# Layer 2 of a four-layer convolution stack: the 17x17 box filter as a running sum on VectorE and one banded matmul, with the squares on ScalarE

## The chip, the cores and the metric

The kernel runs on one core of a Trainium2 chip. A core has a matrix engine (TensorE, in the profile PE for the matmuls and PEld for the loads of the stationary operand), a vector engine (VectorE, DVE), an engine for pointwise functions (ScalarE, ACT), GpSimd (POOL) and SyncE (SP), which here only starts transfers. Each engine runs its own instructions in order, and the engines wait for each other by semaphores. Operands lie in an on-chip memory of 128 partitions (SBUF); TensorE writes its results into PSUM, eight banks of 128 x 512 float32 numbers. The metric is the time of one execution in microseconds (us); lower is better.

## The reference

The input is x, four images of 16 channels of 512 x 512 float32 numbers. Four layers follow each other, and each is `x = x + conv(groupnorm(x))` with its own kind of convolution. Groupnorm has eight groups of two channels, with mean and variance over the group's two whole planes. Layer 0 is a block of dilated convolutions, layer 1 a quantized 3 x 3 convolution, layer 3 a convolution of the two-dimensional spectrum. Layer 2, the one at issue, is a box filter of every channel by itself:

```
k = 2 * r + 1                                  # r = 8, k = 17
kx = full((C, 1, 1, k), 1/k);  ky = full((C, 1, k, 1), 1/k)
x = conv(x, kx, padding=[(0, 0), (r, r)], feature_group_count=C)   # along rows
x = conv(x, ky, padding=[(r, r), (0, 0)], feature_group_count=C)   # down columns
...
x = x + _L2_conv_ref(_gn(x), 8)
```

So every output is the mean of a 17 x 17 neighbourhood of the normalised plane, with zeros beyond the edges, and the plane itself is added to it.

## The kernel before, in words

The layers run one after the other and hand their results over through scratch arrays in DRAM: layer 2 reads `x2` and writes `x3`. Layer 2 is the function `layer2`. It walks over 64 planes, i = 16 b + c for image b and channel c. A plane of 512 x 512 lies in SBUF as a tile of 128 partitions by 4 by 512: partition p and block k hold row 128 k + p.

Per plane there are these steps. `load` brings 1 MB from `x2` (line 1171, tile l2x, four buffers). `normal` applies the scale and bias of the group on ScalarE (line 1177, tile l2n). `first` and `second` each make the sum of 17 in one direction, and both do it with the helper `box` (line 1159): the data are the stationary operand, 128 x 128 at a time, and a band matrix `c_band` of 128 x 144 is streamed through; a matmul contracts over partitions, so the result comes out transposed. `first` therefore yields the transposed plane, summed down its columns; ScalarE copies it from PSUM (line 1188, tile l2y). `second` sums the other direction and turns the plane back. Each pass has four output blocks of four matmuls, and a float32 matmul is two instructions in the profile, so a plane takes 64 matmul instructions on line 1159. For each of its four blocks `second` then adds the plane on VectorE straight from PSUM (line 1199, tile l2o) and takes mean and variance of the sum (line 1200, `bn_stats`); every second plane line 1203 merges them into the group's entry of `mv`. One transfer stores the plane to `x3` (line 1201).

`column_sums` serves layer 3: four matmuls with the three columns of `c_cs` (line 1210) sum the finished plane over its rows with the weights 1, cos and sin, on four strips of 32 columns of the array; ScalarE copies the result (line 1214), and three small transfers store it (line 1216).

The order of the work is written out by hand (`manual_schedule`): what the loop at the end of `layer2` calls first, each engine does first. In round i these are: load plane i+3, `first` of plane i+1, `normal` of plane i+2, `column_sums` of plane i-1, `second` of plane i. Two rounds after the end of an image `group_stats` reduces the image's statistics over the partitions with two small matmuls (line 902) and a chain of short VectorE operations; after the second image `edges` prepares rows for layer 3, one step per round (`advance`). In PSUM the two passes have two banks each, the column sums one, the statistics one, the edge rows two.

Of the kernel before, what the change touches and what calls it, by code (L numbers as in the profile page):

```python
# [13 lines left out]
F32 = mybir.dt.float32  # L14
AF = mybir.ActivationFunctionType
ALU = mybir.AluOpType
AX = mybir.AxisListType
PSUM = bass.MemoryType.PSUM
DRAM = bass.MemoryType.DRAM

P = 128
B, C, H, W = 4, 16, 512, 512
NYB = H // 8
G = 8
# [19 lines left out]


R = 8
BAND = P + 2 * R


HW = W // 2  # L50
# [2 lines left out]
def shape_constants():  # L53

    k = {}
    p = np.arange(P)


    sel = np.zeros((P, G), np.float32)
    sel[p, p % C // 2] = 1  # L60
    k["c_sel_g"] = sel


    k["c_frame_is"] = (p // 4 % 4)[:, None] == np.arange(4)[None]
    k["c_parity"] = (p // 8 % 2)[:, None] == np.arange(2)[None]


    j = np.arange(BAND)
    k["c_band"] = np.where(np.abs(p[:, None] - (j[None] - R)) <= R, np.float32(1.0 / (2 * R + 1)), np.float32(0))


    n = W
    th = 2 * np.pi / n
    i = np.arange(n)
    half = np.arange(n // 2)
    split = np.concatenate([half[0::2], half[1::2]])

    def fold(v):
        lo, hi = v[..., split], v[..., split + n // 2]
        return np.concatenate([lo + hi, lo - hi], -1)  # L80

    cos, sin = np.cos(th * i), np.sin(th * i)
    q = np.stack([np.ones(n), cos, sin], -1)
    k["c_cs"] = np.ascontiguousarray(q.reshape(4, P, 3).transpose(1, 0, 2))
    hk = (2.0 / n) * np.sin(th * (np.outer(np.arange(1, n // 2), i) % n)).sum(0)
    d = (half[None, :] - half[:, None]) % n
    hil = [-(hk[d] + s * hk[(d + n // 2) % n]) for s in (1, -1)]
    k["c_hil"] = np.stack([h[1 - o :: 2, o::2] for h in hil for o in range(2)], 1)
    k["c_tab"] = np.broadcast_to(np.stack([cos, sin])[:, split], (P, 2, n // 2))
    y = 2 * np.arange(4)[None] + (p // C % 2)[:, None]  # L90
    k["c_ycs"] = np.stack([cos[y], sin[y]], 1)
    k["c_pair"] = (p // C % 2)[:, None] == np.arange(2)[None]
    k["c_eye"] = (p % C)[:, None] == np.arange(C)[None]
    k["c_ident"] = np.eye(P)
    bg = np.arange(NBG)[None]
    k["c_sel_bg"] = (bg == p[:, None] // 32 * G + p[:, None] % C // 2) * 1.0
    of = (p[:, None] // 32 == np.arange(B)[None]) / n
    k["c_bmask"] = np.stack([-of, of], 1)


    g = p // C % 4
    re = np.array([[1, 0, 0, 0], [0, 1, 0, 0], [0, 0, 1, 0], [0, 0, 0, -1]])
    im = np.array([[0, 1, 0, 0], [-1, 0, 0, 0], [0, 0, 0, 1], [0, 0, 1, 0]])
    k["c_edge_f"] = np.concatenate([re, im], 1)[g]
    k["c_edge_mask"] = (4 * (p // 64) + np.array([0, 1, 2, 2])[g])[:, None] == p[None] // C
    k["c_edge_sum"] = (g[:, None] < 2) * 1.0
    k["c_third"] = (g[:, None] == 2) * 2.0 * n
    first = (i == 0) * 1.0
    v = np.stack([-cos / n, -sin / n, -np.ones(n) / n, first])
    of = (np.arange(C)[None, :] == (p % C)[:, None])[None, :, None, :]  # L110
    k["c_lc"] = (v[g].reshape(P, NYB, 8).transpose(1, 0, 2)[..., None] * of).reshape(NYB, P, P)
    row = np.zeros((P, 2, n))
    row[g == 3, 0] = fold(first)
    row[g == 3, 1] = -fold(hk)
    k["c_bias_row"] = row
    return {name: np.ascontiguousarray(a, dtype=np.float32) for name, a in k.items()}
# [738 lines left out]
class Kernel:  # L855
# [43 lines left out]
    def across(self, psum, tag, ones, val, n):  # L899

        ps = psum.tile([P, n], F32, name=f"ps_{tag}", tag="gn_ps")
        self.nc.tensor.matmul(ps, ones, val, start=True, stop=True)
        t = self.small.tile([P, n], F32, name=f"ac_{tag}", tag=f"gn_{tag}")
        self.nc.vector.tensor_copy(t, ps)
        return t
# [230 lines left out]
    def layer2(self, x2, x3, sums, gn, l3):  # L1136
        tc, nc = self.tc, self.nc
        res, under_way = [], []
        with ExitStack() as ctx:
            wpool = ctx.enter_context(tc.tile_pool(name="l2w", bufs=1))  # L1140
            xin = ctx.enter_context(tc.tile_pool(name="l2x", bufs=4))
            work = ctx.enter_context(tc.tile_pool(name="l2work", bufs=2))
            edge = ctx.enter_context(tc.tile_pool(name="l2edge", bufs=1))
            ps1 = ctx.enter_context(tc.tile_pool(name="l2p1", bufs=2, space=PSUM))
            ps2 = ctx.enter_context(tc.tile_pool(name="l2p2", bufs=2, space=PSUM))
            pc = ctx.enter_context(tc.tile_pool(name="l2p3", bufs=1, space=PSUM)).tile([P, W], F32, name="l2p3")
            gps = ctx.enter_context(tc.tile_pool(name="l2gps", bufs=1, space=PSUM))
# [1 line left out]
            nc.vector.memset(pc, 0.0)  # L1149
            band, cs = l3.band, l3.cs  # L1150
            mv = wpool.tile([P, B, G, 2], F32, name="mv3")
            xts, xns, yts, outs = {}, {}, {}, {}

            def box(ps, lhs, at):

                for k in range(4):
                    lo, hi = max(0, P * k - R), min(W, P * k + P + R)
                    j = lo - (P * k - R)
                    nc.tensor.matmul(  # L1159
                        ps[:, lo:hi],  # L1160
                        lhs[:, k, at : at + P],
                        band[:, j : j + hi - lo],
                        start=(k == 0),
                        stop=(k == 3),
                        skip_group_check=True,
                    )

            def load(i):
                b, c = divmod(i, C)
                xts[i] = xin.tile([P, 4, W], F32, name=f"l2x_{i}", tag="x")  # L1170
                nc.sync.dma_start(xts[i], x2[b][:, c, :].rearrange("(k p) w -> p k w", p=P))

            def normal(i):
                b, c = divmod(i, C)
                g = c // 2
                xns[i] = work.tile([P, 4, W], F32, name=f"l2n_{i}", tag="xn")
                nc.scalar.activation(  # L1177
                    xns[i], xts[i], AF.Identity, bias=gn[b][1][:, g : g + 1], scale=gn[b][0][:, g : g + 1]
                )

            def first(i):

                xn = xns.pop(i)
                yts[i] = work.tile([P, 4, H], F32, name=f"l2y_{i}", tag="yt")
                for wb in range(4):
                    ps = ps1.tile([P, H], F32, name=f"l2p1_{i}_{wb}", tag="ps")
                    box(ps, xn, wb * P)
                    nc.scalar.copy(yts[i][:, wb, :], ps)  # L1188

            def second(i):  # L1190
                b, c = divmod(i, C)
                yt, xt = yts.pop(i), xts.pop(i)
                o = outs[i] = work.tile([P, 4, W], F32, name=f"l2o_{i}", tag="o", bufs=3)
                if c % 2 == 0:
                    self.st = self.small.tile([P, 2, 4, 6], F32, name=f"st3_{i}", tag="st3")
                for hb in range(4):
                    ps = ps2.tile([P, W], F32, name=f"l2p2_{i}_{hb}", tag="ps")
                    box(ps, yt, hb * P)
                    nc.vector.tensor_add(o[:, hb, :], xt[:, hb, :], ps)  # L1199
                    nc.vector.bn_stats(self.st[:, c % 2, hb, :], o[:, hb, :])  # L1200
                nc.sync.dma_start(x3[b][:, c, :].rearrange("(k p) w -> p k w", p=P), o)
                if c % 2 == 1:
                    nc.vector.bn_aggr(mv[:, b, c // 2, :], self.st.rearrange("p i r s -> p (i r s)"))

            def column_sums(i):

# [11 lines left out]
            def advance():  # L1218
                for e in list(under_way):
                    if next(e, None) is None:  # L1220
                        under_way.remove(e)
# [4 lines left out]
            n = B * C  # L1226
            with tc.manual_schedule():
                for i in range(3):
                    load(i)
                normal(0)  # L1230
                first(0)
                normal(1)
                for i in range(n + 1):
                    if i + 3 < n:
                        load(i + 3)
                    if i + 1 < n:
                        first(i + 1)
                    if i + 2 < n:
                        normal(i + 2)
                    if i > 0:  # L1240
                        column_sums(i - 1)
                    if i < n:
                        second(i)
                    advance()
                    if i > C and i % C == 1 or i == n:
                        b = (i - 1) // C - (i < n)
                        res.append(self.group_stats(gps, self.stats, f"x3_{b}", mv[:, b], G))
                        if b == 1:
                            under_way.append(self.edges(l3, 0, res, sums, tiles, *eps))
# [548 lines left out]
```

## Time and profile before

| | |
|---|---|
| median of 3 runs | 5003.81 us (4993.23 to 5010.5) |
| the profiled execution | 5009.29 us, span 5007.5 us |
| TensorE busy over the span | 4718.3 us, 94% |
| VectorE busy | 4028.1 us, 80% |
| ScalarE busy | 2558.2 us, 51% |
| layer 2, first normalisation to last addition | 3361.4 to 3998.0 us of the span |
| granted clock of TensorE, mean over the span | 0.977 |

The profile is of one execution. Its page gives the busy time of each engine, the chain of work that ended last, and groups of instructions: line, engine, operation, what is written and read by the program's names with partitions x elements, the count, and then busy time and mean duration in nanoseconds, and the idle time of the engine just before them with what ended it. A time line, the chain in order of time, and sums over chosen windows can be asked of the same trace. Matmuls overlap, so the duration of one matmul is longer than the distance to the next. The granted clock is the share of TensorE's full clock that the chip allowed in that time.

Durations of layer 2 before, each from its row: line 1177 2097 ns for 2048 elements, line 1188 586 ns, line 1199 675 ns, line 1200 695 ns, line 1203 372 ns, line 1214 575 ns.

### The profile page before, as it was taken

To read this page: it belongs to the slowest core of one execution; us is meant where nothing else is said; L and a number is where in the kernel's file an instruction comes from. 1 tells how busy PE (TensorE), PEld (TensorE's weight loads), DVE (VectorE), ACT (ScalarE), POOL (GpSimd) and SP (SyncE) were. 2 spreads that over 40 slices of the span, in tenths; PEclk is the share of its full clock that TensorE was granted. 3 is DMA by queue.
4 is the path that set the end of the run, shared out by engine and by line. 5 is a ranking of instruction groups with operands and counts; after the bars stand their busy time and mean duration, and the time that the engine had idled before them with its cause. 6 is when DMAs were issued, how large, how long until landed. Compare 5 with 4: busy or idle time off the path is not lost.

```text
span 5007.5 us, 200506 instructions
## 1 busy us (share of the span) xinstructions
PE 4718.3 (94%) x90224; PEld 2669.6 (53%) x90224; DVE 4028.1 (80%) x4031; ACT 2558.2 (51%) x4156; POOL 21.4 (0%) x90
## 2 busy tenths in 40 slices
PE   4899999999999999989989699989999989999999
PEld 1344444444444444434434345548888767777776
DVE  8888888979779899899899666655555588888887
ACT  3465656563324443444434555545444456666665
POOL 0000000000000000000000000000000000000000
PEclk9999999999999999999999899999999999999999
DMA  5656665563577677776875688866666655555553
GB/s 174 167 159 168 173 167 158 154 177 99 120 143 157 151 158 158 155 161 145 163 151 134 171 267 271 266 227 228 215 215 203 208 137 148 149 143 141 152 147 115
DMA packets 393819, 850.64 MB, mean 170 GB/s; under 512 B 70912, under 2 KB 86400, under 8 KB 384512
## 3 DMA queue, kind: packets, MB, share of 16 engines
q1 hardware_dynamic: 385456, 827.22, 61.9%
q8 instruction: 707, 11.58, 1.1%
q10 hardware_dynamic: 7504, 10.60, 0.8%
q14 instruction: 152, 1.25, 0.1%
HBM read 497.51 MB, written 340.03 MB: 167 GB/s over the span
## 4 chain that ended last, share of the span: by engine, by line
PE 79%; DVE 12%; DMA 3%; issue 3%; ACT 2%; SPq 1%; ACTq 0%; POOL 0%; DVEq 0%; POOLq 0%
PE m L592 41%; PE l1p L1052 10%; PE l2p L1159 8%; PE u L1627 5%; PE s L1568 5%; PE u L1568 4%; DVE frame L500 3%; PE u L1590 2%; PE pt L1602 2%; DVE l2o L1199 2%; PE l2p L1210 1%; DVE frame L445 1%; DVE st L1200 1%; DMA frame<-y 1%; DVE B L641 1%
## 5 line engine op out<-in xcount | busy, mean ns | idle before, releaser
L592 PE MATMUL m<-frame,l0w 32*64 32x512 f32 (+1 forms) x55296 | 2609.5, 611 | 176.1 <-DVE frame L540 63.3
L592 PEld LDWEIGHTS m<-frame,l0w 32*64 32x64 f32 (+1 forms) x55296 | 1178.6, 119 | 1606.0 <-issue 1389.4
L500 DVE SCALAR_TENSOR_TENSOR frame<-frame,frame 128x2376 f32<-128x2376 f32 x232 | 607.9, 2629 | 8.6
L1052 PE MATMUL l1p<-l1q,l_wt 32*32 32x512 f32 (+1 forms) x9216 | 429.6, 604 | 48.0 <-DVE l1q L1039 41.5
L1199 DVE TENSOR_TENSOR l2o<-l2x,l2p 128x512 f32<-128x512 f32 x256 | 172.8, 675 | 263.6 <-PE l2p L1159 263.6
L714 ACT ACTIVATE junk<-xb,neg 128x1024 f32<-128x1024 f32 x256 | 294.1, 1149 | 85.4 <-issue 42.6
L1052 PEld LDWEIGHTS l1p<-l1q,l_wt 32*32 32x32 f32 (+1 forms) x9216 | 189.9, 113 | 249.8 <-issue 209.5
L1159 PEld LDWEIGHTS l2p<-k_c_band,l2y 128*128 128x128 f32 x2048 | 256.7, 190 | 75.8 <-issue 55.0
L1188 ACT COPY l2y<-l2p 128x512 f32<-128x512 f32 x256 | 150.0, 586 | 280.7 <-PE l2p L1159 280.7
L1159 PE MATMUL l2p<-k_c_band,l2y 128*128 128x144 f32 (+1 forms) x2048 | 284.2, 292 | 6.1
L445 DVE STREAM_TRANSPOSE frame<-xp 128x1056 f32<-128x1056 f32 x128 | 261.2, 2124 | 29.7 <-ACT xp L414 29.7
L1159 PE MATMUL l2p<-k_c_band,l2n 128*128 128x144 f32 (+1 forms) x2048 | 266.6, 290 | 13.8 <-DMA l2x<-x 6.8
L1159 PEld LDWEIGHTS l2p<-k_c_band,l2n 128*128 128x128 f32 x2048 | 260.1, 195 | 14.5 <-ACT l2n L1177 12.2
L1627 PE MATMUL u<-k_c_hil,zt 128*128 128x128 f32 x2048 | 255.9, 278 | 0.0
L1627 PEld LDWEIGHTS u<-k_c_hil,zt 128*128 128x128 f32 x2048 | 238.4, 192 | 2.1 <-issue 0.8
L1603 ACT COPY zt<-pt 128x512 f32<-128x512 f32 x256 | 131.4, 599 | 208.2 <-PE pt L1602 208.2
L1533 DVE TENSOR_TENSOR xc<-l3n,k_c_tab 128x2048 f32<-128x2048 f32 x64 | 146.7, 2293 | 107.6 <-ACT l3n L1517 107.6
L1067 ACT ACTIVATE l1o<-l1p,k_l_bias,l_osc 128x1024 f32<-128x1024 f32 x128 | 147.2, 1201 | 144.8 <-PE l1p L1052 139.3
L1646 DVE SCALAR_TENSOR_TENSOR l3o<-u,l3t 128x256 f32<-128x256 f32 x512 | 192.5, 427 | 22.3 <-ACT l3t L1638 19.5
L1069 DVE BATCH_NORM_STATS2 l1st<-l1o 128x6 f32<-128x512 f32 x256 | 158.2, 681 | 54.4 <-ACT l1o L1067 54.2
L1052 PE MATMUL l1p<-l1x,l_wt 32*32 32x512 f32 (+1 forms) x3064 | 195.0, 593 | 0.0
L1033 ACT ACTIVATE l1t<-l1x,l1own,l1own 128x1024 f32<-128x1024 f32 x128 | 151.8, 1234 | 81.4 <-DMA l1x<-x 76.5
(313 smaller groups left out, 6256.7 us busy)
## 6 DMA issues: line engine op xcount, KB each, us to landing
y<-y SPq DMA_DIRECT2D x256, 264.0 KB
xb<-in_x SPq DMA_DIRECT2D x512, 128.0 KB
x<-l1o SPq DMA_DIRECT2D x256, 256.0 KB
l2x<-x SPq DMA_DIRECT2D x64, 1024.0 KB
x<-l2o SPq DMA_DIRECT2D x64, 1024.0 KB
l3x<-x SPq DMA_DIRECT2D x256, 256.0 KB
out<-l3o SPq DMA_DIRECT2D x256, 256.0 KB
l1x<-x SPq DMA_DIRECT2D x252, 256.0 KB
```

Of the source, the lines that this page charges most:

```text
L445: nc.vector.transpose(v[:, :, :, h, 1:17].rearrange("p k u m -> p k m u"), xp)
L500: self.nc.vector.scalar_tensor_tensor(o, x, f, y, ALU.mult, ALU.add)
L592: return nc.tensor.matmul(ps[at, i, :].rearrange("p (k c m) -> p k c m", k=nc_, c=2), w[PX * i : PX * i + PX, weights], source(i, d, e, j) ...
L714: nc.scalar.activation(junk, xs[:, h], f, bias=neg, accum_out=self.out_sums[b][n][:, 2 * t + h : 2 * t + h + 1])
L1033: nc.scalar.activation(t[:, at], x[:, at], AF.Identity, bias=own[1], scale=own[0])
L1052: ins = nc.tensor.matmul(ps[at : at + hi - lo, b, :], wt[rows, d, lo:hi], qs[v % 3][rows, k, d : d + W] if d < 3 else raws[v][rows, k], st ...
L1069: nc.vector.bn_stats(st[b][:, u, :], o[:, b, :])
L1159: nc.tensor.matmul(ps[:, lo:hi], lhs[:, k, at : at + P], band[:, j : j + hi - lo], start=(k == 0), stop=(k == 3), skip_group_check=True,)
L1199: nc.vector.tensor_add(o[:, hb, :], xt[:, hb, :], ps)
L1568: nc.tensor.matmul(ps[b][32 * j : 32 * j + 32], f[rows, n, j, :], x[rows, j, :], start=(i == 0), stop=(i == 2 and tag == "s"), skip_group_ ...
L1627: nc.tensor.matmul(po[:, bass.ts(k, P)], zt[:, b, k ^ 1, :], hil[:, k, :], start=False, stop=(k == 3), skip_group_check=True,)
L1646: nc.vector.scalar_tensor_tensor(o[:, v].rearrange("p k u -> p u k"), po[:, HW:W].rearrange("p (u k) -> p u k", u=2), s, t.rearrange("p (u ...
```

## The change

Layer 2 alone is changed; the rest of the program stays.

- Along the rows: `normal` writes into one of three tiles that are set to zero once. Each of the four rows of a partition takes 520 places there, 512 numbers and 8 zeros, with 17 zeros ahead of the first. `across` makes one VectorE instruction, `tensor_tensor_scan`, over 2080 places: the running value plus the number at this place, minus the number 17 places back. That is the sum of the last 17 numbers; read 8 places later it is centred.
- Down the columns: `down` keeps the band matrix, now 128 x 192 with both factors 1/17 in it, as the stationary operand and streams the row sums, 512 columns at a time. Four full matmuls take the blocks of 128 rows; six of 32 x 32 bring in the 8 rows from the neighbouring block. Nothing is transposed. The two halves of the result lie in two PSUM tiles of two banks each, with two such tiles in all, so the next plane uses the same ones. A plane has 20 matmul instructions here.
- `second` adds the plane with two `tensor_tensor_reduce` instructions of 1024 elements, which also give the sum of the output. ScalarE makes the squares (`Square`, shifted by an approximate mean, with an accumulator) in place of the four copies. `statistics` turns the sums into mean and variance once per image, with six small VectorE operations, in place of `bn_stats` and its merging.
- The order of a round is now: load plane i+3, `normal` of plane i+2, `second` of plane i (with its matmuls), `column_sums` of plane i-1, `across` of plane i+1.

```diff
-            def box(ps, lhs, at):
-                for k in range(4):
...
+            neg = wpool.tile([P, B, G], F32, name="l2neg")
+            for b in range(B):
+                nc.vector.reciprocal(neg[:, b], gn[b][0])
+                nc.vector.tensor_mul(neg[:, b], neg[:, b], gn[b][1])
+            padded = [wpool.tile([P, 2 * R + 1 + 4 * STEP], F32, name=f"l2n_{i}") for i in range(3)]
+            for xn in padded:
+                nc.vector.memset(xn, 0.0)
...
-            def first(i):
...
-                    box(ps, xn, wb * P)
-                    nc.scalar.copy(yts[i][:, wb, :], ps)
+            def across(i):
+                xn = padded[i % 3]
+                h = hs[i] = work.tile([P, 4 * STEP], F32, name=f"l2h_{i}", tag="h")
+                nc.vector.tensor_tensor_scan(
+                    h, xn[:, 2 * R + 1 :], xn[:, 0 : 4 * STEP], 0.0, ALU.add, ALU.subtract
+                )
+
+            def down(i):
+                x = hs.pop(i).rearrange("p (k w) -> p k w", w=STEP)[:, :, R:STEP]
+                ps = [ps2.tile([P, 2, W], F32, name=f"l2p2_{i}_{n}", tag="ps") for n in range(2)]
+                full = slice(0, P)
+                order = [(k, k, full, 32, full) for k in range(4)]
+                for k in range(3):
+                    order.append((k, k + 1, slice(P - 32, P), P + 32, slice(0, 32)))
+                    order.append((k + 1, k, slice(0, 32), 0, slice(P - 32, P)))
+                for k, to, rows, at, out in order:
+                    m = out.stop - out.start
+                    nc.tensor.matmul(ps[to // 2][out, to % 2, :], band[rows, at : at + m], x[rows, k, :],
+                        start=(m == P), stop=True, skip_group_check=True)
+                return ps
...
             def second(i):
...
-                for hb in range(4):
-                    ps = ps2.tile([P, W], F32, name=f"l2p2_{i}_{hb}", tag="ps")
-                    box(ps, yt, hb * P)
-                    nc.vector.tensor_add(o[:, hb, :], xt[:, hb, :], ps)
-                    nc.vector.bn_stats(self.st[:, c % 2, hb, :], o[:, hb, :])
+                for n in range(2):
+                    v = slice(2 * n, 2 * n + 2)
+                    nc.vector.tensor_tensor_reduce(
+                        o[:, v], xt[:, v], ps[n], 1.0, 0.0, ALU.add, ALU.add, s1[:, c, n : n + 1]
+                    )
                 nc.sync.dma_start(x3[b][:, c, :].rearrange("(k p) w -> p k w", p=P), o)
-                if c % 2 == 1:
-                    nc.vector.bn_aggr(mv[:, b, c // 2, :], self.st.rearrange("p i r s -> p (i r s)"))
+                junk = work.tile([P, 4, W], F32, name=f"l2j_{i}", tag="j", bufs=1)
+                nc.scalar.activation(
+                    junk, o, AF.Square, bias=neg[:, b, c // 2 : c // 2 + 1], accum_out=s2[:, c, 0:1]
+                )
...
-                    if i + 1 < n:
-                        first(i + 1)
                     if i + 2 < n:
                         normal(i + 2)
+                    if i < n:
+                        second(i)
                     if i > 0:
                         column_sums(i - 1)
-                    if i < n:
-                        second(i)
+                    if i + 1 < n:
+                        across(i + 1)
+                    if i % C == C - 1:
+                        statistics(i // C)
                     advance()
```

## The prediction

> **What bounds the kernel now.** I read the page first (spans, busy shares, the chain), then cut out the stretch of layer 2 by windows, then the chain inside that stretch, then the groups by shape for prices, and at last short windows around a pause for the granted clock.
>
> ```profile
> span 5007.5 us, 200506 instructions
> PE 4718.3 (94%) x90224; PEld 2669.6 (53%) x90224; DVE 4028.1 (80%) x4031; ACT 2558.2 (51%) x4156; POOL 21.4 (0%) x90
> ```
> ```profile
> 3376.00:3998.00 622.00, 600.87 (x4598) 517.89 (x4596) 357.97 (x612) 301.63 (x380) 0.00 (x0) 0.98 0.65 213
> ```
>
> The second fence is the window of layer 2; its columns are length, busy time and instructions of PE, PEld, DVE, ACT and POOL, granted clock, DMA share, GB/s. TensorE is busy 601 of 622 us, VectorE 358, ScalarE 302, the DMA engines 65%. So TensorE bounds this stretch. The chain says the same; one plane of it, in order of time:
>
> ```profile
> 3404.61 0.70 DVE l2o L1199
> 3405.31 0.02 issue
> 3405.33 0.69 DVE st L1200
> 3406.03 0.60 DVE l2o L1199
> 3406.63 0.04 issue
> 3406.67 5.08 PE l2p L1159 x40
> 3411.75 0.97 PE l2p L1210 x8
> 3412.72 1.17 PE l2p L1159 x8
> ```
>
> A plane takes 9.30 us (the next such piece starts at 3413.91). The 2 us of VectorE in it are a wait for a PSUM buffer that TensorE barely feels: its only stop there is 0.3 us. 64 planes at 9.30 are 595 us; the other 27 us of the window are the breaks for the statistics of an image and the edge rows.
>
> **The order after the change** decides the matter. VectorE runs its instructions in the order written, and per plane i this is now: two reductions of plane i (each with its accumulator read), then the scan of plane i+1. The reductions wait for TensorE's matmuls of plane i; TensorE's matmuls of plane i+1 wait for that scan. Nothing of plane i+1 on TensorE or VectorE can run beside plane i: the path goes round scan, matmuls, reductions, scan. Only the column sums, the ScalarE work and the transfers lie beside it. Before, TensorE had the row sums of plane i+1 to do ahead of the column direction of plane i, and was hardly ever without work. So a plane's time is now a sum over two engines, not the largest of them.
>
> **Prices.**
>
> ```profile
> L445 DVE STREAM_TRANSPOSE frame<-xp 128x1056 f32<-128x1056 f32 x128 | 261.2, 2124 | 29.7 <-ACT xp L414 29.7
> L695 DVE CUSTOM_DVE_ANT_0 xb<-xb,zr 128x2048 f32<-128x2048 f32 x64 | 146.2, 2285 | 7.0 <-DMA xb<-in_x 4.7 <-DMA x<-xb 2.3
> L695 DVE DVE_READ_ACCUMULATOR2_ANT top<- 128x1 f32 x64 | 5.3, 83 | 0.0
> L1379 DVE TENSOR_TENSOR l2edge_xd<-l2edge_x 128x1024 f32<-128x1024 f32 x1 | 1.2, 1208 | 0.0
> ```
> ```profile
> L1439 PE MATMUL po_e<-l3edge_xn,e_f 128*128 128x512 f32 x6 | 2.8, 607 | 0.0
> L1568 PE MATMUL u<-l3n,f 32*32 32x512 f32 x2048 | 138.3, 594 | 0.0
> ```
>
> Added, scan of 128x2080 on VectorE: no row shows one. Low end: L695, the same two-source form, 2048 elements in 2285 ns, gives 2.3 us. High end: L445, the costliest per element, 2124/1056 = 2.01 ns, gives 4.2 us. I take 4.2: each element adds and subtracts on a sum that must be back before the next, two dependent steps, where L695's elements are added independently. Against it stands L1200, whose running moments take 695 ns for 512 elements, the fast rate; 2.3 stays in the range.
>
> [...]
>
> Added, matmuls of a plane: four full ones with 512 columns. L1439 has three such as 6 instructions in 2.8 us, 0.17 of it the last one's tail, so 0.44 each: 8 x 0.44 = 3.5 us. The six 32x32 ones come in pairs on different rows and columns. L1568 runs such tiles at 138.3/2048 = 0.07 us each, so tiles do run side by side; a pair then costs one matmul's two instructions, 3 x 0.88 = 2.6 us. Other end: one after the other, 5.3. I take 2.6, and 0.1 for changing tile shape. Gone are the 64 instructions of L1159 (8.1 us a plane).
>
> Added, reductions: L1379 gives 1.21 us for 1024, plus 0.08 for the read: 1.29 each. Other end: L445's rate, 2.1 each. I take 1.29, since L695 is the same kind of custom operation at the fast rate. The first may start when the second pair is done, 0.9 before the end of the matmuls, and ends 0.4 after it; the second ends 1.7 after it. Gone are four additions and four L1200 (2.7 + 2.8 us), which were hidden.
>
> Handing on between engines: the trace has 0.04 from VectorE to TensorE with 0.19 for the weights, and about 0.2 from the last stream to VectorE. Sum at full clock: scan 4.2 + 0.2 + full matmuls 3.5 + 0.1 + pairs 2.6 + 0.2 + reductions 1.7 = 12.5 us a plane, against 9.30.
>
> **The clock.** In each of these planes TensorE does about 7.2 us (with L1210's 1.0) and then pauses 5.3. Windows of 3.41 us around the pause of 2.6 us for the first image's statistics (clock is the third column from the end):
>
> ```profile
> 3537.06:3540.47 3.41, 0.97 (x8) 0.77 (x7) 3.31 (x7) 0.00 (x0) 0.00 (x0) 1.00 0.14 51
> 3540.47:3543.88 3.41, 2.42 (x10) 2.33 (x11) 1.55 (x11) 0.21 (x1) 0.00 (x0) 0.50 0.99 301
> 3543.88:3547.30 3.42, 3.42 (x16) 3.42 (x16) 0.56 (x4) 1.17 (x2) 0.00 (x0) 0.50 0.84 304
> 3547.30:3550.71 3.41, 3.41 (x28) 2.42 (x28) 0.00 (x0) 2.36 (x3) 0.00 (x0) 1.00 0.00 0
> ```
>
> A window with 0.97 us of work is followed by half the clock; a window busy 2.42 leaves it there, one busy 3.42 lifts it. A pause of 5.3 always leaves a window mostly idle, so each plane's matmuls start at half clock. If the burst begins late in a window, half clock lasts the rest of it and the next; if early, that window's rest alone. Spread evenly, with four windows in five of the first kind, that is 4.4 us, and half of it is lost: 2.2 us a plane (1.4 to 3.1 by position). So 14.7 us a plane.
>
> [...]
>
> **Beside the path.** ScalarE: four copies (4 x 0.59) give way to a square of 2048 (twice L714's 1.15, and 0.19 for its read), about equal; ScalarE has 5.2 of 14.7 us and costs nothing, and would fit even into 7.2. The copy of the column sums now stands behind the square, which waits for the reductions: it ends some 2.9 us after them, and the bank is wanted again a plane later. On SP the three small stores now follow the plane's store, and the load of plane i+4 queues behind them: issued about 4.4 us after the reductions, landing 5.4 us later (first load: issued 3355.8, its reader starts 3361.4), and its reader runs a plane later still. DMA bytes and counts are unchanged, 2 MB over a longer plane. Six small VectorE operations per image lie under the matmuls (1.1 us each time if uncovered).
>
> At the start three memsets of 2097 stand in the chain of layer 1's statistics, 2.0 us each by L1149 (485 ns for 512): the first normalisation moves from 3361.4 to 3364.7, +3.3. At the end the square and those six operations replace L1200 and L1203: +2.8.
>
> **The sum.** Now: first normalisation to last addition is 3361.4 to 3998.0, 636.6 us. After: 3.3 + 2.1 (normalisation) + 64 x 14.7 + 27 (breaks as now) = 973. So 336 + 2.8 = +339. The profiled execution took 5009.3 us (span 5007.5 and 1.8 around it), 5.5 above the median of 5003.8; against the median: 5343, and I say 5345.
>
> **The rivals.**
> Fast scan: 2.3 us. The plane is 10.6 + 2.2 = 12.8, 122 us less: 5223. For it L1200, against it the two dependent steps. Chance 0.15.
> Clock stays up: 12.5 a plane, 141 us less: 5204. Against it the window above; 0.08. With the fast scan too, 10.6: about 5080; 0.03.
> Pairs one by one, or reductions at 2.1: 17.3 or (the second reduction ends 1.8 later) 16.5 a plane, 5511 or 5460. Against them L1568 and L695; 0.12 together.
> Small tiles do not count as busy: no window lifts the clock, the 6.2 us take 12.4, 18.7 a plane, 5600; 0.04.
> Other side: the scan of plane i+1 runs while TensorE works on plane i. Then TensorE's 7.2 us bounds, against VectorE's 6.8, and the end is about 4870. It decides from a plane below 9.3 us. For it: both engines have room. Against it: the written order puts the scan behind reductions that wait. 0.03, and that is also the chance for faster.
>
> **How the numbers follow.** My forecast has 0.55; by the ends of clock loss and scan its own range is 5280 to 5420. The range 5200 to 5490 takes in the fast scan, the steady clock and slow reductions, and leaves out about 0.15. A change under 0.3% (15 us) can't be told from none here; no case ends there, I leave 0.01. Slower is the rest, 0.96.
>
> **What would show it.** Right: in layer 2 VectorE idles before the first reduction for TensorE, TensorE before its first full matmul for the scan, and the two alternate in the chain; the scan's mean is near 4.2 us; the granted clock over the stretch is about 0.8; a plane is near 14.7. Wrong: a scan near 2.3, a granted clock near 1, pairs that start one after the other, or scan and matmuls overlapping in time.

## The result and the profile after

The changed kernel takes 5306.38 us (median of 4 runs, 5299.81 to 5309.53); the kernel before, in the same sitting, 5005.06 us. The ratio is 1.0607, with a 95% interval of 1.059 to 1.0625: 6.1% slower. The profiled execution of the changed kernel has a span of 5307.7 us against 5007.5 before, 300.2 us more.

From the page of the changed kernel, the span and the busy times, then the three groups that layer 2 now consists of (busy us, mean ns of one | idle time of the engine just before them, and what ended it):

```profile
span 5307.7 us, 194596 instructions
PE 4716.3 (89%) x87408; PEld 2353.6 (44%) x87408; DVE 4123.5 (78%) x3842; ACT 2539.4 (48%) x4028; POOL 21.4 (0%) x90
...
L1192 PE MATMUL l2p<-l2h,k_c_band 32*32 32x512 f32 (+1 forms) x1280 | 537.5, 706 | 316.5 <-DVE l2h L1177 300.5
...
L1211 DVE CUSTOM_DVE_ANT_0 l2o<-l2x,l2p 128x1024 f32<-128x1024 f32 x128 | 151.2, 1219 | 478.5 <-PE l2p L1192 478.5
L1177 DVE TENSOR_TENSOR_SCAN l2h<-l2n 128x2080 f32<-128x2080 f32 x64 | 287.1, 4486 | 1.4 <-ACT l2n L1169 1.4
```

The extra work does not account for the loss: TensorE is busy 4716 us against 4718, ScalarE 19 us less, and VectorE 95 us more, in a span that is 300 us longer. What is new stands to the right of the second bar. VectorE idles 478.5 us before the reductions because the matmuls are not done, and TensorE idles 300.5 us before the matmuls because the scan is not done. Each waits for the other, in turn, once per plane.

The same stretch of 622 us that was shown of the kernel before; here layer 2 goes on beyond it (columns: length, busy us of PE, PEld, DVE, ACT, POOL with their instructions, granted clock, DMA share, GB/s):

```profile
3376.00:3998.00 622.00, 405.80 (x1245) 130.36 (x1242) 303.61 (x282) 197.78 (x176) 0.00 (x0) 0.80 0.45 147
```

TensorE fell from 601 to 406 us of the window, at a granted clock of 0.80 instead of 0.98. VectorE fell too, from 358 to 304. Nothing bounds this stretch any more but the sum of the two. One plane in the time line (start, duration, engine, line, operation, count, in brackets the wait before it):

```profile
3496.26 4.49 DVE L1177 TENSOR_TENSOR_SCAN l2h<-l2n 128x2080 f32<-128x2080 f32 x1
...
3500.89 8.00 PE L1192 MATMUL l2p<-l2h,k_c_band 128*128 128x512 f32 x20 [5.14 <-DVE l2h L1177]
...
3508.08 1.22 DVE L1211 CUSTOM_DVE_ANT_0 l2o<-l2x,l2p 128x1024 f32<-128x1024 f32 x1 [7.34 <-PE l2p L1192]
...
3509.23 1.22 DVE L1211 CUSTOM_DVE_ANT_0 l2o<-l2x,l2p 128x1024 f32<-128x1024 f32 x1
...
3510.37 4.49 DVE L1177 TENSOR_TENSOR_SCAN l2h<-l2n 128x2080 f32<-128x2080 f32 x1
...
3515.00 7.77 PE L1192 MATMUL l2p<-l2h,k_c_band 128*128 128x512 f32 x20 [5.14 <-DVE l2h L1177]
```

Read the starts downwards: scan 3496.3, matmuls 3500.9, first reduction 3508.1, second 3509.2, next scan 3510.4. No two of these overlap, except the end of the matmuls with the first reduction and tails of 0.1 us. At full clock such a plane is 4.49 (scan) + 0.15 (to the first matmul) + 3.43 (full matmuls, 8 x 0.429) + 0.09 (change of tile shape) + 2.60 (pairs) + 1.64 (to the next scan) = 12.40 us. The planes between the breaks last 14.51 on average, which is 2.11 more; the run with the pause filled, below, shows that this is the clock.

The clock by windows of 3.41 us through the same plane and the next (the clock records of this trace, but for the last, are whole multiples of 3.413 us long; clock is the third column from the end):

```profile
3493.95:3497.37 3.42, 1.80 (x12) 0.11 (x8) 3.40 (x5) 0.94 (x1) 0.00 (x0) 1.00 0.03 11
3497.37:3500.78 3.41, 0.00 (x0) 0.00 (x0) 3.38 (x1) 3.41 (x4) 0.00 (x0) 0.50 0.82 303
3500.78:3504.19 3.41, 3.30 (x4) 1.51 (x5) 0.00 (x0) 0.22 (x1) 0.00 (x0) 0.50 0.69 174
3504.19:3507.61 3.42, 3.42 (x13) 1.04 (x13) 0.00 (x0) 0.00 (x0) 0.00 (x0) 1.00 0.35 136
3507.61:3511.02 3.41, 2.25 (x14) 0.22 (x10) 2.94 (x5) 0.47 (x1) 0.00 (x0) 1.00 0.00 0
3511.02:3514.43 3.41, 0.00 (x0) 0.00 (x0) 3.41 (x1) 3.41 (x4) 0.00 (x0) 1.00 0.83 310
3514.43:3517.85 3.42, 2.85 (x4) 1.33 (x5) 0.43 (x1) 0.68 (x1) 0.00 (x0) 0.50 0.53 131
```

The second and the third lines are one pattern: a pause at 0.50, and then the first 3.3 us of matmuls also at 0.50. The clock rose after this window, busy 3.30 of 3.41 us, and not after the empty one before it. In the third line four matmul instructions run; in the fourth, thirteen (eight of them small, in pairs).

The +300.2 us add up. From the first scan to the last reduction layer 2 takes 934.1 us (3364.7 to 4298.85): 64 planes of 14.51 are 928.6, which leaves 5.5 for the breaks. With 2.1 for the first normalisation that is 936.2 us, against 636.6 from the same point to the last addition before: +299.6. The first normalisation starts 1.2 later (the three memsets bring 3.15, and layer 1 ended 1.9 earlier in this execution), the statistics of the last image are 2.6 longer, and layer 3 was 3.2 shorter, which was not followed up.

### The profile page after: what moved, and what is told of

The parts are those of the page before. It is cut to its first block, busy times and chain, and to the rows that moved or that the text cites. A ratio compares the mean times of both kernels' runs of the same rounds, so it can differ in the third digit from the quotient of the medians.

```text
span 5307.7 us, 194596 instructions
## 1 busy us (share of the span) xinstructions
PE 4716.3 (89%) x87408; PEld 2353.6 (44%) x87408; DVE 4123.5 (78%) x3842; ACT 2539.4 (48%) x4028; POOL 21.4 (0%) x90
## 5 line engine op out<-in xcount | busy, mean ns | idle before, releaser
L592 PEld LDWEIGHTS m<-frame,l0w 32*64 32x64 f32 (+1 forms) x55296 | 1195.4, 119 | 1590.3 <-issue 1355.6
L1192 PE MATMUL l2p<-l2h,k_c_band 32*32 32x512 f32 (+1 forms) x1280 | 537.5, 706 | 316.5 <-DVE l2h L1177 300.5
L1211 DVE CUSTOM_DVE_ANT_0 l2o<-l2x,l2p 128x1024 f32<-128x1024 f32 x128 | 151.2, 1219 | 478.5 <-PE l2p L1192 478.5
L1192 PEld LDWEIGHTS l2p<-l2h,k_c_band 32*32 32x32 f32 (+1 forms) x1280 | 179.1, 179 | 671.5 <-issue 670.7
L1216 ACT ACTIVATE l2j<-l2o,l2neg 128x2048 f32<-128x2048 f32 x64 | 128.1, 2002 | 627.5 <-DVE l2s L1211 627.5
L1177 DVE TENSOR_TENSOR_SCAN l2h<-l2n 128x2080 f32<-128x2080 f32 x64 | 287.1, 4486 | 1.4 <-ACT l2n L1169 1.4
L1665 ACT ACTIVATE l3t<-u,rr 128x128 f32<-128x128 f32 x512 | 152.4, 362 | 70.2 <-DVE rr L1648 53.4
```

The costliest lines, as they stand in the source:

```text
L592: return nc.tensor.matmul(ps[at, i, :].rearrange("p (k c m) -> p k c m", k=nc_, c=2), w[PX * i : PX * i + PX, weights], source(i, d, e, j) ...
L1177: nc.vector.tensor_tensor_scan(h, xn[:, 2 * R + 1 :], xn[:, 0 : 4 * STEP], 0.0, ALU.add, ALU.subtract)
L1192: nc.tensor.matmul(ps[to // 2][out, to % 2, :], band[rows, at : at + m], x[rows, k, :], start=(m == P), stop=True, skip_group_check=True,)
L1665: nc.scalar.activation(t[:, cols], po[:, cols], AF.Identity, bias=rr[:, b, odd : odd + 1], scale=0.5)
```

## The experiments

The theory on trial: the loss is one serial sum per plane, and it is serial only because VectorE's order holds the scan of plane i+1 behind the reductions of plane i; what the pause costs in clock comes on top. The rival: a price is to blame (a scan that is slow, transfers, the ScalarE work), and the order matters little. All ratios are against the kernel before, run on the same chip.

### The scan ahead of the matmuls and reductions

The loop of the changed kernel, with the same instructions in another order:

```diff
                     if i + 2 < n:
                         normal(i + 2)
+                    if i + 1 < n:
+                        across(i + 1)
                     if i < n:
                         second(i)
                     if i > 0:
                         column_sums(i - 1)
-                    if i + 1 < n:
-                        across(i + 1)
```

> Changed kernel, but each round issues the scan of plane i+1 before the matmuls and reductions of plane i, so the scan stands ahead of reductions that wait for TensorE. Order theory (the changed kernel is slow because scan, matmuls and reductions follow each other): a plane falls from 14.5 us to the largest of TensorE 7.2 and VectorE 4.49 + 2.4 = 6.9, some 7.4 us, with the clock back near 1; layer 2 then takes about 510 us against 637 before the change, and the kernel lands near 4880 us, below both. Price theory (the new instructions themselves are too dear, or transfers cannot follow): at most a small part of the 301 us comes back, the time stays above 5200. Transfers as a limit between the two: 2.1 MB a plane at the 271 GB/s that slices of the first profile reach is 7.8 us a plane, near 4905.

Measured: 4876.74 us (4873.41 to 4885.34), ratio 0.9746 (0.973 to 0.9762). The window of layer 2 and a plane of the time line:

```profile
3376.00:3820.00 444.00, 430.26 (x1652) 130.70 (x1651) 401.05 (x374) 262.65 (x232) 0.00 (x0) 0.98 0.83 274
```
```profile
3702.52 6.39 PE L1192 MATMUL l2p<-l2h,k_c_band 128*128 128x512 f32 x20
3703.09 4.49 DVE L1177 TENSOR_TENSOR_SCAN l2h<-l2n 128x2080 f32<-128x2080 f32 x1
...
3708.10 1.22 DVE L1211 CUSTOM_DVE_ANT_0 l2o<-l2x,l2p 128x1024 f32<-128x1024 f32 x1 [0.52 <-PE l2p L1192]
3708.84 1.04 PE L1235 MATMUL l2p<-l2o,k_c_cs 128*3 128x512 f32 x8
...
3709.82 6.39 PE L1192 MATMUL l2p<-l2h,k_c_band 128*128 128x512 f32 x20
```

Now the scan (3703.1 to 3707.6) lies under the matmuls of another plane (3702.5 to 3708.9). A plane is 7.30 us, all of it TensorE (6.4 of matmuls and 1.0 of column sums, overlapping a little), TensorE is busy 430 of 444 us, and the clock is back at 0.98. The scan still takes 4.49 us; that no longer matters. The order alone is worth 430 us, and with it the change is a gain of 2.5% instead of a loss of 6.1%. The DMA engines are at 0.83 of this window, so the transfers come next: ScalarE waits for a load 13 times in this window, 17.3 us in all, but the planes between the breaks keep to 7.30.

### The pause filled

To take the clock alone out of the sum, five full matmuls per plane that nobody reads, into the PSUM bank of the statistics, issued after the column sums, so that they run while TensorE would wait for the scan:

```diff
+            def fill(i):
+                ps = gps.tile([P, W], F32, name=f"l2f_{i}", tag="gn_ps")
+                for _ in range(5):
+                    nc.tensor.matmul(
+                        ps, l3.ident, l3.tab.rearrange("p n k -> p (n k)"), start=True, stop=True, skip_group_check=True
+                    )
...
                     if i + 1 < n:
+                        fill(i)
                         across(i + 1)
```

> Changed kernel with five more full matmuls per plane (128x128 by 512, constant operands, their result is never read) on TensorE after the column sums, that is 4.3 us of work in its pause of 5.1 us; order unchanged. Clock theory (the pause halves the clock at the start of each plane, 2.1 us lost a plane): the granted clock goes to about 1, a plane falls from 14.5 to 12.4 us, the time by 135 us to about 5171, though TensorE does more. Rival (half clock is not what lengthens the plane, or the extra matmuls get in the way): 5306 or more, up to 5580 if they all lie on the path.

Measured: 5184.16 us (5178.58 to 5191.46), ratio 1.0358 (1.0342 to 1.0375), so 122 us less than the changed kernel, by adding work. The window, and the time line of the pause:

```profile
3376.00:3998.00 622.00, 588.72 (x1910) 201.71 (x1908) 345.74 (x331) 225.98 (x202) 0.00 (x0) 0.99 0.52 169
```
```profile
3500.76 4.56 PE L1233 MATMUL l2f<-k_c_tab,k_c_ident 128*128 128x512 f32 x10
...
3505.97 6.37 PE L1192 MATMUL l2p<-l2h,k_c_band 128*128 128x512 f32 x20 [0.65 <-DVE l2h L1177]
```

The clock is 0.99, the twenty matmul instructions take 6.37 us instead of 8.00, and all planes between the breaks are 12.48 us, against the 12.40 that the parts give at full clock. So the clock's share of the loss is 14.51 - 12.48 = 2.03 us a plane by this run. The expectation was 13 us too low, of which the breaks account for some 9: they cost 14.6 us here and 5.5 in the changed kernel.

### The feedback taken out of the scan

A plain subtraction of the same two operands takes the scan's place, so the running sums are left out and only differences of two numbers remain:

```diff
-                nc.vector.tensor_tensor_scan(
-                    h, xn[:, 2 * R + 1 :], xn[:, 0 : 4 * STEP], 0.0, ALU.add, ALU.subtract
-                )
+                nc.vector.tensor_tensor(h, xn[:, 2 * R + 1 :], xn[:, 0 : 4 * STEP], ALU.subtract)
```

> Changed kernel with the scan replaced by a plain subtraction of the same two inputs into the same output, 128x2080 (so the row sums are left out and the output is not the reference's); order unchanged. Order theory: the scan is on the path, so the plane shortens by 4.49 - 2.32 = 2.2 us at least, 139 us in all, to about 5167; its pause on TensorE falls from 5.1 to 2.9 us, and if that keeps the clock up the plane is about 10.4 and the time near 5045. Rival (the path is elsewhere, the scan lies beside other work): no change, 5290 or more.

Measured: 5111.21 us (5104.43 to 5121.41), ratio 1.0214 (1.0195 to 1.0232). The instruction, by its line (min/median/max ns), and two planes of the time line:

```profile
L1177 DVE TENSOR_TENSOR l2h<-l2n x64: 2318/2320/2326, 3358.5 to 4082.4; 128x2080 f32<-128x2080 f32 x64
```
```profile
3501.20 8.06 PE L1190 MATMUL l2p<-l2h,k_c_band 128*128 128x512 f32 x20 [2.97 <-DVE l2h L1177]
...
3525.03 6.37 PE L1190 MATMUL l2p<-l2h,k_c_band 128*128 128x512 f32 x20 [2.97 <-DVE l2h L1177]
```

2320 ns against 4486: the scan costs 2166 ns more than the plain pass, 1.04 ns for each of 2080 elements. That the feedback is what costs them is argued and not shown by this run, since the subtraction is another instruction and also does one step less. The result lies between the two numbers expected, because the clock did something in between: with the shorter pause (2.97 us instead of 5.14) some planes kept the full clock and some did not (6.37 us for the twenty matmul instructions, or 8.06 and 7.88; granted clock of the stretch 0.90), in a cycle of 10.31, 12.01 and 11.82 us. Neither case had been that.

### Both at once

The subtraction, and two of the idle matmuls per plane to keep the clock up:

```diff
-                nc.vector.tensor_tensor_scan(
-                    h, xn[:, 2 * R + 1 :], xn[:, 0 : 4 * STEP], 0.0, ALU.add, ALU.subtract
-                )
+                nc.vector.tensor_tensor(h, xn[:, 2 * R + 1 :], xn[:, 0 : 4 * STEP], ALU.subtract)
...
+            def fill(i):
+                ps = gps.tile([P, W], F32, name=f"l2f_{i}", tag="gn_ps")
+                for _ in range(2):
+                    nc.tensor.matmul(
+                        ps, l3.ident, l3.tab.rearrange("p n k -> p (n k)"), start=True, stop=True, skip_group_check=True
+                    )
...
                     if i + 1 < n:
+                        fill(i)
                         across(i + 1)
```

> The subtraction in place of the scan (row sums left out, so not the reference's output) together with two extra full matmuls per plane in TensorE's pause, so that the clock stays up; order as in the changed kernel. If scan and clock are separate terms of one serial sum, the plane is that of the filled pause less the scan's surplus, 12.48 - 2.17 = 10.31 us, at every plane alike, and the time 5184 - 139 = 5045. If the two are not additive or something else sets the plane, it lies off this by more than 20 us.

Measured: 5041.96 us (5037.02 to 5050.77), ratio 1.007 (1.0048 to 1.0091).

```profile
3376.00:3998.00 622.00, 557.87 (x1952) 174.57 (x1950) 290.50 (x388) 271.95 (x242) 0.00 (x0) 1.00 0.62 203
```

Clock 1.00, and every plane between the breaks 10.31 us. That is 12.48 - 10.31 = 2.17 us less than with the scan, the 2166 ns by which the scan is dearer, to the last digit that these numbers have. So the terms of the sum add, as serial terms do: 14.51, less 2.03 for the clock, less 2.17 for the scan. The two prices together are most of the loss, yet neither alone brings the kernel back to 5005 us (5184 and 5111), and with both gone it is still 0.7% slower than before. That they count at all is the order's doing: with the scan ahead, and at the same price, the loss is gone.

### The squares alone

The kernel before, with only the statistics of the change: the addition and its sum in one instruction (four of 512 here, since PSUM is as before), the squares on ScalarE, and the six operations per image. The two matmul passes and the copies stay.

```diff
-                    nc.vector.tensor_add(o[:, hb, :], xt[:, hb, :], ps)
-                    nc.vector.bn_stats(self.st[:, c % 2, hb, :], o[:, hb, :])
+                    nc.vector.tensor_tensor_reduce(
+                        o[:, hb, :], xt[:, hb, :], ps, 1.0, 0.0, ALU.add, ALU.add, s1[:, c, hb : hb + 1]
+                    )
...
-                if c % 2 == 1:
-                    nc.vector.bn_aggr(mv[:, b, c // 2, :], self.st.rearrange("p i r s -> p (i r s)"))
+                junk = work.tile([P, 4, W], F32, name=f"l2j_{i}", tag="j", bufs=1)
+                nc.scalar.activation(
+                    junk, o, AF.Square, bias=neg[:, b, c // 2 : c // 2 + 1], accum_out=s2[:, c, 0:1]
+                )
...
+                    if i % C == C - 1:
+                        statistics(i // C)
```

> Kernel before, with only the third part of the change: additions that also give the sum (four of 512 elements a plane), squares on ScalarE in place of the statistics on VectorE. In the kernel before VectorE is not the limit, so nothing is to be gained: 5005 if the squares hide. They stand on ScalarE ahead of the copies that the next row sums need for their PSUM banks; if those wait, up to 1.2 us a plane, 77 us, is lost: 5080. Rival (VectorE's statistics did hold TensorE up): below 4990.

Measured: 5075.99 us (5073.67 to 5078.8), ratio 1.0143 (1.0126 to 1.016), at the upper end of what was expected, and in part by luck: a plane takes 10.80 us instead of 9.30, 1.5 where 1.2 was put, which is 96 us over 64 planes, but the breaks for the statistics and the edge rows cost some 12 us here against 33 in the kernel before (counted in the part on why). Why, by the waits of the stretch (engine, tile and line that wait, for whom: us in total, times, longest):

```profile
ACT l2j L1209 <- DVE l2s L1204: 174.8, 60, 4.3
...
PE l2p L1163 <- ACT l2y L1192: 89.3, 57, 3.2
```

And in the time line:

```profile
3502.66 2.00 ACT L1209 ACTIVATE l2j<-l2o,l2neg 128x2048 f32<-128x2048 f32 x1 [2.92 <-DVE l2s L1204]
3504.66 1.05 ACT L1192 COPY l2y<-l2p 128x512 f32<-128x512 f32 x2
...
3505.28 2.17 PE L1163 MATMUL l2p<-k_c_band,l2n 128*128 128x136 f32 x16 [1.54 <-ACT l2y L1192]
```

It is the same fault on another engine. The square waits for the last reduction of plane i; the copies of plane i+1, which TensorE needs next, are queued behind it on ScalarE. TensorE stops 1.54 us for them in the plane shown, about the 1.50 us by which it is longer. In the changed kernel there are no such copies, and in its layer 2 TensorE has no wait for ScalarE in the list of waits. This part of the change is harmful with the old pass and harmless with the new one.

### The scan ahead, with the old statistics

The reordered kernel with the statistics of the kernel before on VectorE:

```diff
-                    nc.vector.tensor_tensor_reduce(
-                        o[:, v], xt[:, v], ps[n], 1.0, 0.0, ALU.add, ALU.add, s1[:, c, n : n + 1]
-                    )
+                    nc.vector.tensor_add(o[:, v], xt[:, v], ps[n])
...
-                nc.scalar.activation(
-                    junk, o, AF.Square, bias=neg[:, b, c // 2 : c // 2 + 1], accum_out=s2[:, c, 0:1]
-                )
+                for hb in range(4):
+                    nc.vector.bn_stats(self.st[:, c % 2, hb, :], o[:, hb, :])
+                if c % 2 == 1:
+                    nc.vector.bn_aggr(mv[:, b, c // 2, :], self.st.rearrange("p i r s -> p (i r s)"))
```

> The version with the scan issued ahead (4877 us), but with the statistics as in the kernel before: two plain additions of 1024 and four statistics instructions of 512 on VectorE, no squares on ScalarE. If VectorE becomes the limit: scan 4.49 + two additions 2.3 + four statistics 2.6 = 9.4 us a plane or somewhat more where TensorE's pauses cost clock, against 7.3; 5010 to 5080 us. If instead the squares on ScalarE bring nothing here, as alone in the kernel before: 4877 or less.

Measured: 4985.72 us (4978.11 to 4992.1), ratio 0.9962 (0.9949 to 0.9976).

```profile
3376.00:3820.00 444.00, 377.28 (x1348) 116.41 (x1347) 435.16 (x405) 125.01 (x98) 0.00 (x0) 0.93 0.67 224
```
```profile
3558.91 4.48 DVE L1177 TENSOR_TENSOR_SCAN l2h<-l2n 128x2080 f32<-128x2080 f32 x1
3563.30 2.33 DVE L1210 TENSOR_TENSOR l2o<-l2x,l2p 128x1024 f32<-128x1024 f32 x2
...
3565.55 2.47 DVE L1213 BATCH_NORM_STATS2 st<-l2o 128x6 f32<-128x512 f32 x4
...
3568.05 0.37 DVE L1215 BATCH_NORM_AGGREGATE mv<-st 128x2 f32<-128x48 f32 x1
```

Here VectorE is the bound, busy 435 of 444 us; the four lines are a whole plane of it, 9.43 us until the next scan, and the mean of planes with and without the last line is 9.2. That is about the 9.30 of the kernel before: the scan alone, well placed, brings next to nothing, because the statistics fill VectorE. So the squares on ScalarE are worth 109 us once the scan is ahead, and the two halves of the change need each other. The time was below the expected range: a plane is 9.2 us where the range began at 9.4, which is 13 us in all, the breaks cost some 25 us against 33 before, and the clock loss that the range allowed for, a granted clock of 0.93 here, does not show in a plane that VectorE bounds.

## Why the prediction was right, and where it was off

**The order.** Right, and shown. The path round scan, matmuls and reductions is in the time line, with nothing of two planes overlapping, and moving one call by two lines removes it. The two waits named as the sign of it are 478.5 us (VectorE for TensorE) and 300.5 us (TensorE for VectorE). That the two alternate in the chain of waits is not shown: the chain covers 18% of the span, all of it in layer 3. The time line shows the alternation. The rival in which the scan runs beside the matmuls was priced at about 4870 us and refused for the written order; with the order changed it came out at 4877.

**The scan.** Taken at 4.2 us, measured 4.486. The reason given, two dependent steps per element, was the author's estimate: it fits the measured 4486 ns against 2320 for the subtraction of the same 2080 elements, a ratio of 1.93, and no run tested it by itself. The row that 4.2 came from is a transpose, another operation altogether: it was near by size, not by likeness. The forecast's own range of 5280 to 5420 us is also wider than the clock losses of 1.4 to 3.1 us a plane make it (about 5290 to 5400); no run shows a term for the rest, and the scan as measured, 0.29 us above 4.2, is 18 us over 64 planes.

**The matmuls and reductions.** Full matmuls 3.43 for 3.5. The pairs do run side by side, with starts 6 ns apart: 2.60 for 2.6. From the last pair to the next scan 1.64 where 0.2 + 1.7 was forecast, since the reductions take 1219 ns and 83 for the read but start 1.14 apart. In sum 12.40 where 12.5 was written; the scan's +0.29 and the smaller handing-on cancel.

**The clock.** 2.2 us a plane forecast, 2.11 by the parts and 2.03 by the filled pause. The granted clock of the stretch is 0.80, as said. The method, a mean over evenly spread positions, was lucky: the positions are not evenly spread (below). A window need not be idle for the clock to fall. The pause of 5.14 us often holds a wholly idle window, and 29 of the clock's 62 falls in layer 2 come right after one. The other 33 come after a window with some work in it, 0.24 to 1.87 us, as the first drop in the table above does: it follows a window with 1.80 us of work, at the start of the idle one and not at its end. With the subtraction the pauses of 2.97 us are shorter than a window, and the clock still falls: 0.90 over the stretch.

**The breaks.** This is the step that failed: "27 (breaks as now)". They cost 5.5 us, so 21.5 of the 39 us by which the forecast was too high are from here. Before, the breaks were six planes of 12.0 to 16.5 us instead of 9.30, around the statistics of an image and the edge rows. They stand 33 us above 9.30, not 27: the 27 came from taking 64 planes off a window at whose start the first pass of two planes was already done. Four of these six held a wait of TensorE, 3.5 to 4.4 us, and then 3.4 or 6.8 us at a granted clock of 0.50; the two of 12.0 and 13.7 us held neither. In the changed kernel every plane already contains such a wait, and 62 of 64 start at a granted clock of 0.50, so there is little for a break to add: its break planes are 16.5, 17.2 and 16.8 against a mean of 14.5, and one among the edge rows is only 12.5. The kernel with the squares alone, with a wait of 1.5 us in each plane, pays some 12, the one with the filled pause, which has the clock to lose again, 14.6, and the reordered one, whose planes hardly wait, 29. I carried over a cost of a state that the change abolishes. This reading is drawn from these totals; no run varied the breaks by themselves.

**The rest of the sum.** The planes (14.51 for 14.7) are 12 us of the difference; 1.9 are from layer 1 and 3.2 from layer 3 in this execution. The start (+3.15 for +3.3) and the end (+2.6 for +2.8) were as forecast.

## What to carry to other kernels

On an engine that runs its instructions in order, put what feeds the next item ahead of what waits for the present one; the same instructions gave 5306 us in one order and 4877 in the other, and the square ahead of the copies was the same fault on ScalarE. Before blaming a price, ask whether it is a term of a sum or one of several that a maximum is taken over: the scan's 4.49 us is all loss in the one order and free in the other. And a cost that is carried over from the kernel before holds only while the state that it disturbs is still there.

## What the runs showed of the hardware

The scan of 2080 elements took 1.93 times as long as a plain pass: 4486 ns against 2320 for a subtraction of the same elements, 1.04 ns more per element.

The planes repeat in step with the clock's windows. In the changed kernel they do not scatter around 14.51 but repeat every four: 13.88, 15.47, 14.57, 14.11, together 58.03 us, which is 17 windows of 3.413 us. With the subtraction the time line has 12.01, 11.82 and 10.31, together 34.14 us, 10 windows, and the next plane begins as the first of them did: the distance of its weight loads grows from 0.43 to 0.81 us at the same place, 1.4 us in. The author's reading is that a plane that gains full clock early ends early, its successor begins at another place in its window, and after a whole number of windows it all comes round. It fits the traces; no run was made to vary it. The loss goes with it: at the pause of 5.14 us it is 2.03 us a plane, at 2.97 us it is 1.07, since one plane in three then escapes it and the other two lose 1.5 and 1.7. Other lengths of the pause were not run.

The table of clock windows in the section on the result has both sides of the fall: after a window busy 1.80 of 3.42 us the clock drops, and after one busy 2.25 of 3.41 it stays. Small tiles were enough for that: the window busy 2.25 us holds nothing but 32 x 32 matmuls and the column sums, three columns wide. Busy time alone does not draw the line, though. In the run with the subtraction the distance of the weight loads (0.43 us at full clock, 0.85 at half) changes near 3502.6 and 3516.25 us, four windows apart. Counted from there, the window that ends at 3502.6 has 1.40 us of full matmuls and is followed by half clock; the one from 3523.1 to 3526.5 has 1.47 us of them and nothing else, and the clock stays. In the changed kernel 1.80 us of small tiles and column sums were not enough. What does draw the line was not followed up.
